# Denominators of a lookup-table convolution by tensor tiles of 128 rows and 32 columns, with the two accumulator banks told apart by the set of logits

## The chip, the cores and the metric

The kernel runs on one core of one Trainium2 chip. The metric is the device time of one execution in microseconds, the median of three runs. A profiled execution on the same chip gives the trace from which all durations here are read.

## The reference

The input is 16 images of 256 channels with 28 x 28 pixels. After a group normalization (32 groups) it passes twice through a "lookup" convolution, each with a batch normalization behind it; then a gate per channel (squeeze and excitation), a residual sum, a rectifier and the outer residual sum follow. The convolution is what matters here:

```python
def amm_conv3x3(x, centroids, w_sub):              # centroids: C x k x s = 256 x 16 x 9
    p = patches(x, 3, 3)                           # B, n, C, s: nine taps of each channel
    d = sum(p * p) - 2 * einsum('bncs,cks->bnck', p, centroids) + sum(centroids * centroids)
    attn = softmax(-d, axis=-1)                    # over the k = 16 centroids of a channel
    lut = einsum('cks,cso->cko', centroids, w_sub)
    return einsum('bnck,cko->bno', attn, lut)
```

For each channel and pixel a softmax over 16 centroids is taken. Its weighted sum of the centroids has nine taps, and these go through an ordinary matrix product with `w_sub`. The kernel computes it in that order: logits, exponentials, numerators for nine taps and a denominator, the quotient, and the product over channels and taps. All of it is fp32.

## The kernel before, in words

**Blocks.** The work is cut into 128 blocks: two layers, 16 images, and for each image two halves of the channels (128 each) by two halves of the rows (14 rows, N = 392 pixels). A block holds four sets of logits, `mm` = 0 to 3, and each set has four groups `i` with 128 partitions: 8 channels with 16 centroids each. So one block has 4 x 4 x 8 = 128 channels.

**Steps of a block.** `logits` (line 613) makes a set of logits with 16 matmuls on tiles of 32 rows and 32 columns. `exps` (line 624, ScalarE) writes the exponentials `e`. `num_b` (line 678) makes, from all four sets, the denominators and the ninth tap's numerators in the accumulator pair `nb`. `num_a` (line 664) makes the other eight taps in the pairs `na`, one pair for each set. `product` (line 748) multiplies the scaled numerators `qp` (eight taps) and `qo` (ninth tap) with the weights into `acc`, with full 128x128 tiles.

**The denominators.** `nb` has two banks. In both, 32 rows belong to each group `i`: 16 of them are ninth-tap numerators and 16 are denominators. Which bank has its numerators in the lower 16 and which in the upper 16 rows differs, so that each bank gives one half of each. `split_r` (line 688, ScalarE) takes the upper rows of bank 0 with a mask. `join_r` (line 692, VectorE) adds the lower rows of bank 1: together these are the denominators `r`. `recip_dve` (line 706) inverts them. `split_q` and `join_q` (lines 698 and 703) collect the ninth tap's numerators from the other halves in the same way. `spread` (lines 717 and 721) copies the reciprocals to the rows of the numerators with a shuffle in 32 partitions whose pattern `mask_of` gives. `scale_a`, `copy_a` and `scale_q` then multiply.

Before the change the two banks are told apart by the half of the 128 rows, that is, by the channels of a group: rows 0 to 63 of the exponentials go to bank 0, rows 64 to 127 to bank 1, and each bank accumulates over all four sets. `rows_of` gives the place of each channel in these rows. The constants, the mask tables and the table that places the second layer's weights are laid out by it.

**Order.** Each engine works through its own list, which the program writes by hand: `at(step, sub, ...)` puts a call at a place, and the calls are issued in order of these places. For most blocks TensorE's order in a double step is logits, denominators, logits, products, logits, numerators, logits, products. The denominators thus lie between two logits stages. Accumulator pairs come from a ring of four pairs. In the blocks of the second layer with the first channel half the first set takes a longer way with a subtracted maximum.

Of the kernel before, what the change touches and what calls it, by code (L numbers as in the profile page):

```python
# [23 lines left out]
N = RT * W  # L24
# [57 lines left out]

def rows_of(m, c, a):
    r, c4, mm = c >> 1, 2 * (c & 1) + a, m & 3
    return r, c4, mm, 16 * r + 4 * mm + c4, 16 * (1 - r) + 4 * mm + c4


@with_exitstack
def kernel(
# [22 lines left out]
    nc = tc.nc  # L112
# [19 lines left out]
    def fixed(u, kind):  # L132
        return None if u["step"] is None else EARLY.get((kind, u["step"] // 2))

    def banks(name, step=None, role=None, tag=None):
        if tag is not None:
            pass
        elif step is None:
            spin[0] = (spin[0] + 1) % 4
            tag = spin[0]  # L140
        else:
            tag = (role - step // 2) % 4
        return p_ring.tile([P, 2, 512], F32, tag=f"ps{tag}", name=name)
# [4 lines left out]
    def after(u, n):  # L148
        return None if u["step"] is None else u["step"] + n
# [49 lines left out]
    wts = {}  # L199
# [472 lines left out]
    def num_b(u):  # L672
        bs = banks("nb", after(u, 2), ROLES["nb"], fixed(u, "nb"))
        for mm in range(4):
            es = u["e", mm]
            for i in range(4):
                for r in range(2):
                    nc.tensor.matmul(  # L678
                        bs[32 * i : 32 * i + 32, r, :N],
                        lhsT=wts["cwb", u["hh"]][64 * r : 64 * r + 64, mm, i, :],  # L680
                        rhs=es[64 * r : 64 * r + 64, i, :],
                        start=(mm == 0), stop=(mm == 3),
                    )
        u["nb"] = bs

    def split_r(u):
# [21 lines left out]
    def mask_of(k):  # L708
        if k == 8:
            return [(xx + 16) % 32 for xx in range(32)]  # L710
        mm, r = divmod(k, 2)
        return [16 * (1 - r) + 4 * mm + (xx >> 3) for xx in range(32)]

    def spread(u, mm):
        if mm == 4:
            rb = rpool.tile([P, N], F32, tag="rb1", name="rb1", bufs=1)
            nc.vector.stream_shuffle(rb, u["r"], mask_of(8))  # L717
        else:
            rb = rpool.tile([P, 2, N], F32, tag="rb", name="rb", bufs=4)
            for r in range(2):  # L720
                nc.vector.stream_shuffle(rb[:, r, :], u["r"], mask_of(2 * mm + r))  # L721
        u["rb", mm] = rb
# [527 lines left out]
    for j, u in enumerate(blocks):  # L1250
# [3 lines left out]
        for p in range(2):  # L1254
# [6 lines left out]
            for q in range(2):  # L1261
                mm = 2 * p + q
# [11 lines left out]
        kept = () if j == 1 else SLOT_MM[1 : 4 if wide_next(j) or j == 0 else 2 : 2]  # L1274
        g = 2 * j + 1 + (j > 2)
        at(g, 1.0, num_b, u)
        at(g, 1.05, split_r, u)
        at(g, 1.2 if j > 1 else 1.055, join_r, u)
# [158 lines left out]
    for o in range(2):  # L1437
# [7 lines left out]
        for part in range(2):  # L1445
            c = 40 + 8 * o + 2 * part
# [5 lines left out]
    for part in range(3):  # L1452
        c = (68, 70, 76)[part]
# [96 lines left out]
    with tc.If(rv > 0):  # L1550
        with tc.For_i(0, B, 1) as it:
# [14 lines left out]
            for l in range(2):  # L1566
# [6 lines left out]
                for t2 in range(2):  # L1573
                    us = []
                    for hh in range(2):
                        u = {"l": l, "b": B, "t": t2, "hh": hh, "w": 0, "step": None}
                        for k in range(5):
                            u["qi", k] = hh if k == 4 else 4 * hh + k
                        us.append(u)
                        for mm in range(4):  # L1580
                            if mm % 2 == 0:
                                u["pt", mm // 2] = pts[mm // 2]
                                patches(u, mm // 2)
                            logits(u, mm)
                            wide_copy(u, mm)
                            wide_turn(u, mm)
                            wide_max(u, mm)
                            wide_sub(u, mm)
                            wide_back(u, mm)
                            wide_exp(u, mm)  # L1590
                        num_b(u)
                        split_r(u)
                        join_r(u)
                        split_q(u)
                        join_q(u)
                        recip_dve(u)
                        spread(u, 4)
                        scale_q(u, 4)
                        for mm in range(4):
                            spread(u, mm)  # L1600
                            num_a(u, mm)
                            scale_a(u, mm)
# [23 lines left out]
def _lay_out(inputs):  # L1626
# [15 lines left out]
    for c0 in range(ch):  # L1642
        i, a, m, c = digits(c0)
        r, c4, mm, rn, rs = rows_of(m, c, a)
        hh = m >> 2
        ka = slice(32 * c + 16 * a, 32 * c + 16 * a + 16)
        for s in range(S):
            wd[32 * i + 16 * a + tap_row(s), m, c, 16 * a : 16 * a + 16] = cent[c0][:, s]
        cwa[ka, m, i, 8 * c4 : 8 * c4 + 8] = cent[c0][:, :8]
        cwb[ka, m, i, rn] = cent[c0][:, 8]  # L1650
        cwb[ka, m, i, rs] = 1.0
        ws[32 * i + 8 * c4 : 32 * i + 8 * c4 + 8, NS * hh + 2 * mm + r] = wsub[c0, :8]
        ws[32 * i + rn, NS * hh + 8] = wsub[c0, 8]
        konst[ka, 3 + c4] = 1.0
        konst[ka, 48 + 32 * mm + rn] = 1.0
        konst[ka, 176 + 32 * mm + rs] = 1.0
        wa = (2 * m + r) * 16 + 4 * i + c4
        ids[c0] = (c0, (2 * c + a) * 32 + 4 * m + i, 2 * wa, 2 * wa + 1, hh * P + 32 * i + rn, 2 * c0, 2 * c0 + 1)
# [66 lines left out]
```

## Time and profile before

| what | value |
|---|---|
| time, median of 3 runs | 2607.75 us (2605.92 to 2608.51) |
| the profiled execution: span | 2606.2 us |
| granted TensorE clock | 0.999 |
| TensorE matmuls busy | 2591.2 us (99%) |
| VectorE, ScalarE, GpSimd busy | 1776.6, 1371.7, 1905.6 us |
| DMA | 372.07 MB, mean 143 GB/s |
| line 748 `product`, records of matmuls with qp and `wall` | 3088 records, 1097.5 us |
| line 613 `logits` | 15872 records, 469.0 us |
| line 664 `num_a` | 8192 records, 376.5 us |
| line 678 `num_b` | 8192 records, 375.2 us |

The profiled execution's span of 2606.2 us, from its first to its last instruction, is the only time known of it; it lies 1.5 us below the median of the runs. An fp32 matmul appears as two records in the trace, one for each of its two passes. Records of several tiles overlap in time, and "busy" is the length of their union. In a row of the timeline stand the start, the length of the union, the engine, the line, the operands, the tile (64*32 is 64 rows by 32 columns of the array) and the number of records. A row of the groups ends with busy time, the mean duration of one record in ns, and the engine's idle time before the group's records with what ended it.

### The profile page before, as it was taken

How to read it: one execution, taken by the hardware profiler on the slowest of the kernel's cores; microseconds unless marked ns; L12 is line 12 of the kernel's file. 1: busy time of each engine (PE TensorE's matmuls, PEld its weight loads, DVE VectorE, ACT ScalarE, POOL GpSimd, SP SyncE). 2: the span in 40 equal slices, each digit the busy share in tenths (PEclk: the TensorE clock that was granted, in tenths of full speed). 3: DMA queues.
4: the chain of work that ended last, by engine and by line, in shares of the span. 5: the costliest groups of instructions: out<-in, count | busy, mean ns of one | idle time of the engine just before them, and what ended most of it. 6: DMA issues, size and time to landing. Idle time of an engine off the chain costs nothing.

```text
span 2606.2 us, 85832 instructions
## 1 busy us (share of the span) xinstructions
PE 2591.2 (99%) x37026; PEld 1273.2 (49%) x37026; DVE 1776.6 (68%) x3797; ACT 1371.7 (53%) x1913; POOL 1905.6 (73%) x1341
## 2 busy tenths in 40 slices
PE   8999999999999999999999999999999999999999
PEld 4444455444454444544444444444444444444445
DVE  8766656666657666566676767766776667767676
ACT  6444444444444445444445555555555655555565
POOL 6687666776567776667666887878878787787786
PEclk9999999999999999999999999999999999999999
DMA  7556656565545575564664444444344444444442
GB/s 228 166 131 184 195 166 187 160 168 170 163 141 147 157 194 173 165 172 134 176 169 103 109 112 127 119 119 120 101 126 128 118 116 112 115 124 128 117 104 66
DMA packets 213288, 372.07 MB, mean 143 GB/s; under 512 B 29496, under 2 KB 183528, under 8 KB 212328
## 3 DMA queue, kind: packets, MB, share of 16 engines
q1 hardware_dynamic: 206584, 333.75, 47.6%
q0 software_dynamic: 6176, 32.66, 3.5%
q8 instruction: 295, 4.83, 0.8%
q14 instruction: 89, 0.73, 0.1%
q10 hardware_dynamic: 144, 0.10, 0.0%
HBM read 288.46 MB, written 77.95 MB: 141 GB/s over the span
## 4 chain that ended last, share of the span: by engine, by line
PE 99%; ACT 0%; POOL 0%; DVE 0%; issue 0%; DMA 0%; POOLq 0%; ACTq 0%
PE acc L748 52%; PE lg L613 17%; PE na L664 14%; PE nb L678 14%; ACT e L624 0%; PE sep L1049 0%; POOL qp L757 0%; PE sep L1041 0%; DMA xt<-in_x 0%; PE tap L392 0%; PE sqp L374 0%; PE sqp L343 0%; POOL qp L729 0%; PE gnp L534 0%; PE gnp L551 0%
## 5 line engine op out<-in xcount | busy, mean ns | idle before, releaser
L748 PE MATMUL acc<-qp,wall 128*128 128x392 f32 (+1 forms) x3088 | 1097.5, 498 | 0.3 <-POOL qp L757 0.2
L624 ACT ACTIVATE e<-lg 128x784 f32<-128x784 f32 x960 | 737.8, 820 | 635.2 <-PE lg L613 632.0
L757 POOL TENSOR_TENSOR qp<-qp,qp 128x784 f32<-128x784 f32 x512 | 943.7, 1867 | 152.0 <-DVE qp L740 151.6
L748 PEld LDWEIGHTS acc<-qp,wall 128*128 128x128 f32 x3088 | 567.4, 190 | 504.8 <-issue 53.6
L721 DVE STREAM_SHUFFLE rb<-r 128x392 f32<-128x392 f32 x1024 | 551.5, 606 | 0.0
L613 PE MATMUL lg<-pt,wd 32*32 32x392 f32 x15872 | 469.0, 499 | 0.2
L692 DVE SCALAR_TENSOR_TENSOR r<-nb,kst,r 128x392 f32<-128x392 f32 x128 | 80.1, 626 | 447.6 <-ACT r L688 447.6
L664 PE MATMUL na<-e,cwa 64*32 64x392 f32 x8192 | 376.5, 493 | 0.0
L740 DVE TENSOR_TENSOR qp<-na,rb 128x784 f32<-128x784 f32 x352 | 334.0, 972 | 62.2 <-PE na L664 50.3
L678 PE MATMUL nb<-e,cwb 64*32 64x392 f32 x8192 | 375.2, 492 | 0.1
L729 POOL TENSOR_TENSOR qo<-qo,rb 128x392 f32<-128x392 f32 x128 | 132.5, 1035 | 297.0 <-DVE rb L717 296.2
L706 DVE RECIPROCAL r<-r 128x392 f32<-128x392 f32 x128 | 333.2, 2603 | 4.4
L729 POOL TENSOR_TENSOR qp<-qp,rb 128x784 f32<-128x784 f32 x160 | 295.7, 1858 | 2.9
L678 PEld LDWEIGHTS nb<-e,cwb 64*32 64x32 f32 x8192 | 191.5, 106 | 174.7 <-issue 24.5
L664 PEld LDWEIGHTS na<-e,cwa 64*32 64x32 f32 x8192 | 183.8, 106 | 184.0 <-issue 74.8
L613 PEld LDWEIGHTS lg<-pt,wd 32*32 32x32 f32 x15872 | 116.4, 103 | 266.6 <-issue 238.3
L748 PE MATMUL acc<-qp,w_A 128*128 128x392 f32 x512 | 182.4, 499 | 0.0
L688 ACT ACTIVATE r<-nb,kst 128x392 f32<-128x392 f32 x128 | 86.7, 678 | 165.5 <-PE nb L678 162.3
L648 POOL TENSOR_TENSOR z<-z,mx 128x1568 f32<-128x1568 f32 x32 | 91.8, 2869 | 94.8 <-DVE mx L642 94.8
L748 PE MATMUL acc<-qo,wall 128*128 128x392 f32 (+1 forms) x386 | 157.9, 491 | 0.0
L734 ACT COPY qp<-na 128x784 f32<-128x784 f32 x160 | 130.0, 813 | 23.6 <-PE na L664 22.1
L748 PEld LDWEIGHTS acc<-qp,w_A 128*128 128x128 f32 x512 | 94.6, 190 | 82.5 <-DVE qp L740 19.8
(241 smaller groups left out, 1706.4 us busy)
## 6 DMA issues: line engine op xcount, KB each, us to landing
pt<-home SPq DMA_DIRECT2D x744, 209.0 KB
pt<-home SPq DMA_DIRECT2D x744, 104.5 KB
home<-xpad SPq DMA_DIRECT2D x30, 899.0 KB
xt<-in_x SPq DMA_DIRECT2D x30, 784.0 KB
out_dram<-y SPq DMA_DIRECT2D x31, 392.0 KB
pt<-in_p SPq DMA_DIRECT2D x6, 784.0 KB
d_wS<-st SPq DMA_DIRECT2D x12, 192.0 KB
wall<-d_wS SPq DMA_DIRECT2D x4, 576.0 KB
```

Source lines behind the costliest of these rows:

```text
L613: nc.tensor.matmul(bk[32 * c : 32 * c + 32, :N].rearrange("p (r w) -> p r w", w=W), lhsT=(wx[u["hh"]] if early(u) else wts["wd", u["hh"]]) ...
L624: nc.scalar.activation(eg[:, 2 * i : 2 * i + 2, :], bk[:, :, :N], AF.Exp, scale=2.0)
L648: nc.gpsimd.tensor_tensor(zk, zk, mx.unsqueeze(2).to_broadcast([P, N // 4, K]), ALU.subtract)
L664: nc.tensor.matmul(bs[32 * i : 32 * i + 32, r, :N], lhsT=wts["cwa", u["hh"]][64 * r : 64 * r + 64, mm, i, :], rhs=es[64 * r : 64 * r + 64, ...
L678: nc.tensor.matmul(bs[32 * i : 32 * i + 32, r, :N], lhsT=wts["cwb", u["hh"]][64 * r : 64 * r + 64, mm, i, :], rhs=es[64 * r : 64 * r + 64, ...
L706: nc.vector.reciprocal(u["r"], u["r"])
L721: nc.vector.stream_shuffle(rb[:, r, :], u["r"], mask_of(2 * mm + r))
L729: nc.gpsimd.tensor_tensor(q, q, u.pop(("rb", mm)), ALU.mult)
L734: nc.scalar.copy(pair(u, mm), u.pop(("na", mm))[:, :, :N])
L740: nc.vector.tensor_mul(pair(u, mm), u.pop(("na", mm))[:, :, :N], rb)
L748: nc.tensor.matmul(accs[key][:, : cols[1] - cols[0]], lhsT=wl[w][:, k, :], rhs=us["q", k][:, cols[0] : cols[1]], start=first and n == 0, s ...
L757: nc.gpsimd.tensor_tensor(pair(out_u, mm), pair(in0, mm), pair(in1, mm), ALU.subtract)
```

## The change

`num_b` issues one matmul with all 128 rows for each set and group, where it issued two with 64 rows each. Sets 0 and 1 go to bank 0, sets 2 and 3 to bank 1, and each bank accumulates over its two sets. `rows_of` and `mask_of` lay out rows and shuffle patterns for this. The masks of `split_r`, `join_r`, `split_q` and `join_q`, the number of shuffles and the order of the calls stay.

```diff
 def rows_of(m, c, a):
     r, c4, mm = c >> 1, 2 * (c & 1) + a, m & 3
-    return r, c4, mm, 16 * r + 4 * mm + c4, 16 * (1 - r) + 4 * mm + c4
+    rn = 8 * mm + 2 * c + a
+    return r, c4, mm, rn, (rn + 16) % 32
...
         for mm in range(4):
             es = u["e", mm]
             for i in range(4):
-                for r in range(2):
-                    nc.tensor.matmul(
-                        bs[32 * i : 32 * i + 32, r, :N],
-                        lhsT=wts["cwb", u["hh"]][64 * r : 64 * r + 64, mm, i, :],
-                        rhs=es[64 * r : 64 * r + 64, i, :],
-                        start=(mm == 0), stop=(mm == 3),
-                    )
+                nc.tensor.matmul(
+                    bs[32 * i : 32 * i + 32, mm >> 1, :N],
+                    lhsT=wts["cwb", u["hh"]][:, mm, i, :], rhs=es[:, i, :],
+                    start=mm % 2 == 0, stop=mm % 2 == 1,
+                )
         u["nb"] = bs
...
         mm, r = divmod(k, 2)
-        return [16 * (1 - r) + 4 * mm + (xx >> 3) for xx in range(32)]
+        return [(8 * mm + 4 * r + (xx >> 3) + 16) % 32 for xx in range(32)]
```

## The prediction

> **What bounds the kernel now.** I read the page's busy shares and chain first, then the waits of TensorE, then the groups by line for the denominators (line 678), then the timeline around one of their stages.
>
> ```profile
> PE 2591.2 (99%) x37026; PEld 1273.2 (49%) x37026; DVE 1776.6 (68%) x3797; ACT 1371.7 (53%) x1913; POOL 1905.6 (73%) x1341
> PE acc L748 52%; PE lg L613 17%; PE na L664 14%; PE nb L678 14%; ACT e L624 0%; PE sep L1049 0%; POOL qp L757 0%; PE sep L1041 0%; DMA xt<-in_x 0%; PE tap L392 0%; PE sqp L374 0%; PE sqp L343 0%; POOL qp L729 0%; PE gnp L534 0%; PE gnp L551 0%
> ...
> PE gnp L436 <- DVE gn_mv L425: 5.6, 1, 5.6
> ...
> PE acc L748 <- POOL qp L757: 0.2, 1, 0.2
> ```
>
> TensorE is busy 2591.2 of 2606.2 us, and the chain that ends last lies on it almost throughout; 14% of it are the denominators. The last two rows are the first and the last of eight in TensorE's own waits. The largest, 5.6 us, falls before the first denominators; the other seven are 0.7 us or less. So a change pays only through the time that TensorE itself takes for the edited stage, and whatever another engine gains or loses up to several us per block stays under that cover.
>
> ```profile
> L678 PE MATMUL nb<-e,cwb x8192: 486/489/515, 21.0 to 2563.7; 64*32 64x392 f32 x200
> 1020.37 0.94 PE L613 MATMUL lg<-pt,wd 32*32 32x392 f32 x32
> 1021.24 2.92 PE L678 MATMUL nb<-e,cwb 64*32 64x392 f32 x64
> 1024.09 0.94 PE L613 MATMUL lg<-pt,wd 32*32 32x392 f32 x32
> ```
>
> The first row gives 8192 records: 128 blocks with 64 each, two passes of each of 32 fp32 matmuls, 0.49 us long in the median and up to 0.51 in a first pass. One stage goes from 1021.24 to the next stage's start at 1024.09: 2.85 us, with logits on both sides. Windows that end inside this stage show how it is built:
>
> ```profile
> 1021.24 0.55 PE L678 MATMUL nb<-e,cwb 64*32 64x392 f32 x4
> 1021.24 0.62 PE L678 MATMUL nb<-e,cwb 64*32 64x392 f32 x8
> 1021.24 0.94 PE L678 MATMUL nb<-e,cwb 64*32 64x392 f32 x16
> 1021.24 1.27 PE L678 MATMUL nb<-e,cwb 64*32 64x392 f32 x24
> ...
> 1023.57 0.59 PE L678 MATMUL nb<-e,cwb 64*32 64x392 f32 x8
> 1037.63 0.53 PE L678 MATMUL nb<-e,cwb 64*32 64x392 f32 x4
> 1037.63 0.56 PE L678 MATMUL nb<-e,cwb 64*32 64x392 f32 x8
> ```
>
> Eight records, one on each tile, take 0.62 us together, sixteen 0.94, twenty-four 1.27. So eight 64x32 tiles run side by side, and each further pass on all of them costs 0.33 us. A stage is eight such passes. Besides them it holds two fixed pieces: the ladder, by which the eighth tile starts after the first (0.62 less one record of 0.51: 0.11 us), and the emptying of the array before the next shape (the last eight start at 1023.57 and the logits at 1024.09: 0.52, less the ladder's 0.11, so 0.41). At 1037.63 the ladder is shorter, 0.56 less 0.51: 0.05.
>
> **The change, part by part.** *The matmuls.* Per block 32 matmuls of 64 rows become 16 of 128 rows: 32 records in place of 64. But four tiles of 128x32 fill the array where eight of 64x32 did, so the passes stay at eight: 16 x 2 records over 4 tiles, 8 x 0.33. Halving the instructions therefore does not halve the stage. What shrinks is the ladder, from eight tiles to four. If the steps stay as they are, four tiles end where the first four do today: 0.62 - 0.55 = 0.07 us less per stage. With even steps of 0.11/7 = 0.015 it is four steps less, 0.06. I take 0.065. In the short form it is 0.56 - 0.53 = 0.03.
>
> How many stages have which form?
>
> ```profile
> 1000.00:2000.00 1000.00, 146.25 (x3208) 74.92 (x3204) 1.00 0.50 135
> ```
>
> In this row (line 678 alone; the stretch, its length, then the busy time of TensorE with its records) 3208 records are 50.1 stages, and 146.25 / 50.1 = 2.92 us each, the long form's busy time. Short ones are rare; I take 8 of 128, an estimate. The sum: 120 x 0.065 + 8 x 0.03 = 8.0 us. From the profiled 2606.2 us that leaves 2598.2. The three runs have a median of 2607.75, 1.5 us above that span, so the forecast is 2599.8.
>
> The trace has no neighbouring 128x32 tiles, so the step between them is unknown. Low end: the short form's step, 0.05/7 = 0.007, three of them 0.02, a gain of 0.09 per long stage and 0.03 per short one, 11.0 us in all, 2596.7. High end: twice the long step, as the rows double, 3 x 0.03 = 0.09, a gain of 0.02, 2.6 us, 2605.2. I take the middle one because the step already differs between two stages of the same shape: the shape does not set it, the arrival of instructions does, and that should not slow down with half as many.
>
> *Weight loads.* They fall from 64 to 32 per block. Per load:
>
> ```profile
> L678 PEld LDWEIGHTS nb<-e,cwb 64*32 64x32 f32 x8192 | 191.5, 106 | 174.7 <-issue 24.5 <-ACT y L779 10.2 <-ACT se_gt L1055 8.9
> L1041 PEld LDWEIGHTS sep<-ysum,w_sb 128*32 128x32 f32 x68 | 3.3, 110 | 8.9 <-issue 8.4 <-DVE ok L1208 0.6
> L748 PEld LDWEIGHTS acc<-qp,wall 128*128 128x128 f32 x3088 | 567.4, 190 | 504.8 <-issue 53.6 <-POOL qp L757 21.3 <-DVE qp L740 20.4
> 1021.24 0.24 PEld L678 LDWEIGHTS nb<-e,cwb 64*32 64x32 f32 x16 [0.64 <-ACT hpad L779]
> 1008.24 1.48 PE L748 MATMUL acc<-qp,wall 128*128 128x392 f32 x4
> ```
>
> A 128x32 load is already in the program, in the gate's small matmuls: 110 ns against 106. Loads lie under matmuls: sixteen of a denominator stage are through after 0.24 us, while the second passes that need half of them start only at 0.94 - 0.62 = 0.32 us or later. I cost them at nothing; the cover is the 0.33 us of the pass before.
>
> The Trainium skill speaks against this cover ("TensorE: Matmul & The Clock Gate", Part 3, The mechanism): a weight load overlaps matmuls in flight "only when row_grp differs", and four tiles of 128 rows share all row groups. By that rule the sum would not be a gain of 8.0 us but the loss of the second rival below. The trace does not bear it out: the products use all rows, each load takes 190 ns, and yet four records fit in 1.48 us, (1.48 - 0.49) / 3 = 0.33 us apart.
>
> *The denominators' earlier half.* Bank 0 now closes after sets 0 and 1, and its copy on ScalarE (line 688) needs nothing more.
>
> ```profile
> 1021.36 1.54 ACT L624 ACTIVATE e<-lg 128x784 f32<-128x784 f32 x2 [0.35 <-PE lg L613]
> 1024.21 0.68 ACT L688 ACTIVATE r<-nb,kst 128x392 f32<-128x392 f32 x1 [1.31 <-PE nb L678]
> 1024.92 0.62 DVE L692 SCALAR_TENSOR_TENSOR r<-nb,kst,r 128x392 f32<-128x392 f32 x1 [8.65 <-ACT r L688]
> ```
>
> Bank 0 is whole after four passes, about 1021.24 + 0.35 + 2 x 0.33 + 0.04 + 0.49 = 1022.8. ScalarE is in the exponentials until 1022.9, so the copy can move from 1024.21 to 1022.9; the join on VectorE then waits for bank 1, ready at about 1024.1, not for 1024.92. The reciprocal chain comes up to 0.8 us earlier per block. If the wait still covers both banks, nothing moves. Both are worth nothing at TensorE, which waits for no reciprocal in the list of its waits; the seven short waits together would be under 5 us and none names this chain. No wait is added, and the first write into bank 1 moves from the first matmuls to the ninth, which only loosens its wait.
>
> *The rest* has one answer, nothing: the spreading keeps its 1024 shuffles with other masks, the constants change their contents and not their sizes, and the scattered rows of the ninth tap's weights go to other places in transfers of the same count. The numerators keep their 64x32 tiles.
>
> **Rivals.** *The ladder's step doubles with the rows.* For: the profile has no 128x32 neighbours. Against: steps of 0.007 and 0.015 in one shape. Time 2605.2, 0.1% less, which is inside what a measurement of this kernel can tell from no change (0.2%, 5.2 us).
>
> *Loads are exposed.* If a load has to stand ahead of its matmul on every pass, a stage pays 8 x 0.11 = 0.88 us, 128 stages 112.6, less 8.0: 2712.4, slower. It decides from 0.065 / 8 = 0.008 us per pass on. For it: four loads of one row group have never stood beside each other here at full height. Against: the 16 loads in 0.24 us and the products above.
>
> *The column tiles take turns.* If only one 128x32 tile streams at a time, a stage has 32 passes instead of 8: 24 x 0.33 = 7.9 us more, 1014 in all, less 8.0: 3614. Two at a time give 8 more passes, 2.64 us, 338 in all: 2938. A fifth of one extra pass per stage is enough to turn the sign. For it: the only 128x32 tile in the trace stands alone. Against: the logits, where all four columns of a row group stream different data at once.
>
> ```profile
> 1024.09 0.61 PE L613 MATMUL lg<-pt,wd 32*32 32x392 f32 x16
> ```
>
> Sixteen tiles, four columns by four rows, take 0.61 us together, so four column streams over all 128 rows are sustained. The Trainium skill lists 128x32 as a shape with four tiles ("TensorEngine Tiling (Array Packing)", Available Configurations); no run here shows it.
>
> **How the numbers follow.** The shorter ladder 0.74; the doubled step 0.13; exposed loads 0.07; turns 0.06. The first lies over 0.2% faster with its ends of 0.06 to 0.09 per stage, the second is the same, the last two are slower: 0.74, 0.13, 0.13. The predicted time is the first's, 2599.8. The range takes both ends of the step, 2596.7 and 2605.2, and 1.5 us at either end, which is how far the runs lie from the span: 2595.2 to 2606.7. It leaves out the two slower rivals, 0.13.
>
> **What would show it.** Right: 4096 records of 128x32 at line 678, still about 0.49 us each, four of them in 0.55 us and eight in 0.88; a stage of 2.78 to 2.79 us from its first start to the next stage; the numerators still 2.85 and the products unchanged; the copy at line 688 over 1 us ahead of where it stood, with no gain from that. Wrong: passes more than 0.33 us apart (loads or turns), a first group of four that takes 0.60 us (the step), or a wait of TensorE that today's list does not have.

## The result, and the profile after

| | before | after |
|---|---|---|
| median time | 2607.52 us (2603.88 to 2608.51, 5 runs) | 2596.91 us (2596.11 to 2598.35, 5 runs) |
| ratio | | 0.9965 (95%: 0.9954 to 0.9976) |
| span of the profiled execution | 2606.2 us | 2595.0 us |

The change makes the kernel 0.35% faster, 9.1 us of 2607.5, where 8.0 us were forecast. By the medians it is 10.6, by the two profiled spans 11.2 us.

First the page of the changed kernel: busy times and the groups of denominators (line 678) and numerators (line 665 there). Each group's row ends with the number of records, their joint busy time and the mean of one in ns.

```profile
PE 2579.0 (99%) x32930; PEld 1215.7 (47%) x32930; DVE 1775.9 (68%) x3797; ACT 1371.8 (53%) x1913; POOL 1906.5 (73%) x1341
...
L665 PE MATMUL na<-e,cwa 64*32 64x392 f32 x8192 | 373.9, 492 | 0.0
L678 PE MATMUL nb<-e,cwb 128*32 128x392 f32 x4096 | 366.3, 495 | 0.1
...
L678 PEld LDWEIGHTS nb<-e,cwb 128*32 128x32 f32 x4096 | 135.1, 109 | 222.2 <-issue 154.4
```

TensorE lost 12.2 us of busy time; the other engines changed by less than 1 us each. The denominators have 4096 records for 8192, each about as long as before (495 against 492 ns on average), and yet their busy time fell only from 375.2 to 366.3 us: half the instructions, the same eight passes. That is 8.9 of the 12.2 us. Another 2.6 us are the numerators', from 376.5 to 373.9, which the change leaves alone; the part on the prediction's total comes back to them. A weight load took 109 ns, close to the 110 of the gate's load.

Next the timeline of TensorE around one such stage of the changed kernel, whole and through windows that end inside it.

```profile
1014.96 0.94 PE L614 MATMUL lg<-pt,wd 32*32 32x392 f32 x32
1015.83 2.86 PE L678 MATMUL nb<-e,cwb 128*32 128x392 f32 x32
1018.62 0.94 PE L614 MATMUL lg<-pt,wd 32*32 32x392 f32 x32
...
1015.83 0.55 PE L678 MATMUL nb<-e,cwb 128*32 128x392 f32 x4
1015.83 0.88 PE L678 MATMUL nb<-e,cwb 128*32 128x392 f32 x8
```

And the stretch from 1000 to 2000 us for line 678 alone: the stretch, its length, the busy time of TensorE and of its weight loads, each with the number of records, then the clock and the DMA.

```profile
1000.00:2000.00 1000.00, 142.87 (x1600) 52.75 (x1600) 1.00 0.51 136
```

The stage goes from 1015.83 to 1018.62, 2.79 us for 2.85. Its first four records take 0.55 us together: four 128x32 tiles run side by side, and the fourth starts 0.04 us after the first, as did the fourth of eight before. The next four add 0.33 us, one pass. In the stretch a stage is busy 142.87 / 50 = 2.86 us, against 2.92: 0.06 us less, and 128 x 0.06 = 7.7 us. Read to the nanosecond, the median stage falls from 2851 to 2788 ns and its ladder from 106 to 39.

Now the timeline of ScalarE and VectorE around the same stage of the changed kernel:

```profile
1015.96 1.54 ACT L625 ACTIVATE e<-lg 128x784 f32<-128x784 f32 x2 [0.36 <-PE lg L614]
1018.74 0.68 ACT L687 ACTIVATE r<-nb,kst 128x392 f32<-128x392 f32 x1 [1.25 <-PE nb L678]
1019.45 0.62 DVE L691 SCALAR_TENSOR_TENSOR r<-nb,kst,r 128x392 f32<-128x392 f32 x1 [8.59 <-ACT r L687]
```

ScalarE is through with the exponentials at 1017.5, and bank 0 is whole at about 1017.4. Still the copy waits 1.25 us, to 0.12 us behind the stage's end. It did not move.

### The profile page after: what moved, and what is told of

It is laid out like the page before. It is cut to its first block, busy times and chain, and to the rows that moved or that the text cites. A ratio compares the mean times of both kernels' runs of the same rounds, so it can differ in the third digit from the quotient of the medians.

```text
span 2595.0 us, 77640 instructions
## 1 busy us (share of the span) xinstructions
PE 2579.0 (99%) x32930; PEld 1215.7 (47%) x32930; DVE 1775.9 (68%) x3797; ACT 1371.8 (53%) x1913; POOL 1906.5 (73%) x1341
## 4 chain that ended last, share of the span: by engine, by line
PE 98%; DVE 1%; ACT 0%; POOL 0%; issue 0%; DMA 0%; POOLq 0%; ACTq 0%
PE acc L747 53%; PE lg L614 17%; PE na L665 14%; PE nb L678 14%; ACT e L625 0%; PE sep L1048 0%; POOL qp L756 0%; PE sep L1040 0%; DMA xt<-in_x 0%; DVE rb L720 0%; DVE r L705 0%; PE tap L393 0%; PE sqp L375 0%; PE sqp L344 0%; POOL qp L728 0%
## 5 line engine op out<-in xcount | busy, mean ns | idle before, releaser
L665 PE MATMUL na<-e,cwa 64*32 64x392 f32 x8192 | 373.9, 492 | 0.0
L678 PE MATMUL nb<-e,cwb 128*32 128x392 f32 x4096 | 366.3, 495 | 0.1
L678 PEld LDWEIGHTS nb<-e,cwb 128*32 128x32 f32 x4096 | 135.1, 109 | 222.2 <-issue 154.4
```

The lines of the kernel that those rows point to most:

```text
L665: nc.tensor.matmul(bs[32 * i : 32 * i + 32, r, :N], lhsT=wts["cwa", u["hh"]][64 * r : 64 * r + 64, mm, i, :], rhs=es[64 * r : 64 * r + 64, ...
L678: nc.tensor.matmul(bs[32 * i : 32 * i + 32, mm >> 1, :N], lhsT=wts["cwb", u["hh"]][:, mm, i, :], rhs=es[:, i, :], start=mm % 2 == 0, stop= ...
```

## Experiments

The kernel before ran beside each of these on the same chip; ratios are to it. Where no ratio is given, the kernel was executed once. For comparison, the changed kernel has 0.9965.

**A second trace of the kernel before.** No edit.

> The kernel before once more, for a second trace. If the stalls in mid-stage (TensorE without an instruction, 0.2 to 0.9 us each, some dozen in the first trace, about 5 us in all) are fixed by the program, they stand at the same blocks; if they are a matter of the execution, at others, with a similar sum. The regular stages stay at 2.85 us for denominators and numerators.

Measured: 2604.58 us, span 2603.1, 3.1 us less than the first trace. The groups of its page:

```profile
L664 PE MATMUL na<-e,cwa 64*32 64x392 f32 x8192 | 374.5, 492 | 0.2 <-issue 0.2
L678 PE MATMUL nb<-e,cwb 64*32 64x392 f32 x8192 | 374.0, 492 | 0.1
```

A logits stage takes 0.94 us in the timeline where nothing stops it. One that does stall, in the first trace:

```profile
1035.87 1.83 PE L613 MATMUL lg<-pt,wd 32*32 32x392 f32 x32
```

And two in the timeline of the second trace:

```profile
548.77 1.74 PE L613 MATMUL lg<-pt,wd 32*32 32x392 f32 x32
1032.49 1.81 PE L613 MATMUL lg<-pt,wd 32*32 32x392 f32 x32
```

Neither outcome that was expected: some stalls come back at the same stage (1.83 and 1.81 us, the block near 1035), some do not, and their sum changes. Summed over all stages between 80 and 2500 us, as what each is longer than the median of its kind with the same neighbours, they are 5.1 us in the first trace and 3.1 in the second; 2.7, 2.9 and 4.1 in the traces of the changed kernel and of the next two experiments. Single spans therefore differ by 2 or 3 us without any edit, and 11.2 us from one pair of them overstates the gain.

**Bank 0 closes last.** From the changed kernel:

```diff
-        for mm in range(4):
+        for mm in (2, 0, 3, 1):
             es = u["e", mm]
```

> The changed kernel, with the four sets of the denominators issued in the order 2, 0, 3, 1, so that bank 0 is whole only with the stage's last matmuls and its copy on ScalarE can start no earlier than in the kernel before. Theory A (the whole gain is TensorE's: a ladder of four tiles in place of eight, and less besides that does not hang on the copy): stage 2.79 us, time as the changed kernel's, 2597 within 2 us, and the 1 us that the numerators of the first block gained at the start stays. Theory B (the earlier copy of bank 0 helps): the copy falls back to over 1 us after ScalarE's exponentials, the early blocks lose what they gained and the time goes up by 1 to 3 us, to 2598 to 2600.

Measured: 2595.64 us against 2604.30, ratio 0.9965 (0.9952 to 0.9979). The timeline of TensorE and of ScalarE in this kernel, a stage and what follows it:

```profile
1015.38 2.86 PE L678 MATMUL nb<-e,cwb 128*32 128x392 f32 x32
1018.16 0.94 PE L614 MATMUL lg<-pt,wd 32*32 32x392 f32 x32
...
1018.28 0.68 ACT L687 ACTIVATE r<-nb,kst 128x392 f32<-128x392 f32 x1 [1.25 <-PE nb L678]
```

The time is the changed kernel's, as theory A has it. But the copy stands 0.12 us behind the stage here as there, so this run took nothing away: it shows that the order of the sets is free, and not what an earlier copy is worth. The 1 us at the start stayed as well: the first stage of numerators goes from 28.64 to 31.43, 2.79 us, against 4.11 in the first trace of before.

**The numerators with their row halves outside.** From the changed kernel:

```diff
-        for i in range(4):
-            for r in range(2):
+        for r in range(2):
+            for i in range(4):
                 nc.tensor.matmul(
                     bs[32 * i : 32 * i + 32, r, :N],
                     lhsT=wts["cwa", u["hh"]][64 * r : 64 * r + 64, mm, i, :],
```

> The changed kernel with the numerators' 64x32 matmuls issued with the row halves outside and the four groups inside; same tiles, same passes. Theory A (the ladder's step is the arrival of instructions at the array, 0.0166 us for each fp32 matmul): the ladder stays at 0.11 us, the stage at 2.85, the time at 2597 within 2. Rival (the step is set by which tile follows which, 7 ns within a group of columns and more from one group to the next, or the reverse): the ladder of the numerators changes to 0.05 or to 0.15 and the time by 7 us either way.

Measured: 2595.83 us against 2604.30, ratio 0.9966 (0.9952 to 0.9980). The first eight numerator records of a stage in this kernel's timeline:

```profile
1026.11 0.62 PE L665 MATMUL na<-e,cwa 64*32 64x392 f32 x8
```

0.62 us, a ladder of 0.11, as before. For these tiles, which one follows which does not set the step; the rival falls.

**Half of the logits moved behind the denominators**, in the kernel before and in the changed one. Of set 0, groups 2 and 3 are made behind the denominators:

```diff
-    def logits(u, mm):
-        bs = []
+    def logits(u, mm, half=None):
+        bs = u.pop(("lg", mm)) if half == 1 else []
...
-        for i in range(4):
+        for i in range(4) if half is None else range(2 * half, 2 * half + 2):
...
+                if mm == 0 and j >= 4 and not wide:
+                    for h in range(2):
+                        at(cl, 1.09 if h else sub, logits, u, mm, h)
+                        at(cl, 1.095 if h else sub + 0.01, exps_half, u, mm, h)
+                    continue
```

> The kernel before, with half of the logits of set 0 (groups 2 and 3, 8 of the 16 matmuls ahead of the denominators) moved behind the denominators, in all blocks but the first four and those that subtract the maximum. It costs passes of its own (about 0.6 us in each such block), so its time is not the question. Theory A (the array's queue holds the logits until they are done, and what comes behind them arrives at 0.0166 us for each matmul): with half as many ahead the first eight denominator matmuls are in the queue, ladder 0.05 us and stage 2.79 in these blocks; 0.11 and 2.85 in the others; the numerators keep 0.11. Rival (the change of shape after logits, or the shape itself, makes the step): 0.11 and 2.85 in all of them.

> The same move of half the logits in the changed kernel. Theory A: the ladder of four tiles falls from 0.04 to 0.02 us and the stage from 2.79 to 2.77 us in these blocks. Rival: 0.04 and 2.79 everywhere.

Measured: 2690.56 and 2685.17 us, 86 us or more over the kernels without the move: some 0.95 us for each of the 91 halved blocks, more than the 0.6 that was expected. What counts are the ladders. The timeline of the edited kernel before: the halved logits, the first eight denominators behind them, and the first eight numerators of another stage with all sixteen logits ahead.

```profile
1016.71 0.89 PE L613 MATMUL lg<-pt,wd 32*32 32x392 f32 x16
1017.52 0.56 PE L684 MATMUL nb<-e,cwb 64*32 64x392 f32 x8
1029.18 0.62 PE L670 MATMUL na<-e,cwa 64*32 64x392 f32 x8
```

And the first four denominators behind halved logits in the timeline of the edited changed kernel:

```profile
1014.84 0.54 PE L684 MATMUL nb<-e,cwb 128*32 128x392 f32 x4
```

Same shape, same neighbour, same kernel: with eight logits matmuls ahead, eight tiles are under way in 0.56 us, with sixteen in 0.62. Read to the nanosecond from the trace, all 91 halved stages have a median ladder of 47 ns and a length of 2794 ns, the 34 with sixteen logits ahead 106 and 2851. In the changed kernel the halved stages have 20 ns and 2776, the others 39 and 2787.

The halved logits differ from the whole ones in one thing more: they leave half of the array's rows without work. That is not the reason, as one stage of numerators in the timeline of the changed kernel shows. It stands straight behind products, which use all 128 rows, and its first eight records take 0.56 us too:

```profile
56.92 4.22 PE L747 MATMUL acc<-qp,wall 128*128 128x392 f32 x12
60.97 0.82 PE L747 MATMUL acc<-qo,wall 128*128 128x392 f32 x2
61.72 0.56 PE L665 MATMUL na<-e,cwa 64*32 64x392 f32 x8
```

So the ladder is set by what stands ahead, not by the shape or its change. That the queue keeps the logits until they are done is the explanation that fits; the trace does not show the queue.

**The matmuls cut in two halves of 196 pixels**, from the changed kernel, first with the two halves of a tile one after the other, then with the four tiles inside. Both have 64 records per block again.

```diff
             for i in range(4):
+                for c0 in (0, N // 2):       # second kernel: this loop outside, i inside
                     nc.tensor.matmul(
-                    bs[32 * i : 32 * i + 32, mm >> 1, :N],
-                    lhsT=wts["cwb", u["hh"]][:, mm, i, :], rhs=es[:, i, :],
-                    start=mm % 2 == 0, stop=mm % 2 == 1,
+                        bs[32 * i : 32 * i + 32, mm >> 1, c0 : c0 + N // 2],
+                        lhsT=wts["cwb", u["hh"]][:, mm, i, :], rhs=es[:, i, c0 : c0 + N // 2],
+                        start=mm % 2 == 0 and c0 == 0, stop=mm % 2 == 1 and c0 > 0,
```

> The changed kernel with every 128x32 denominator matmul cut into two of 196 pixels: again 32 matmuls and 64 records per block, as before the change, but on four tiles. Theory A (the ladder is what the change shortened): a record costs some 2 to 3 ns beside its pixels, 8 x 0.003 us per stage, 3 us in all; stage 2.81 us, ladder still 0.04 us or less, ratio to the kernel before 0.9975 to 0.998. Theory B (half as many instructions is what pays): ratio 1.000, as before the change. Theory C (stalls in mid-stage come with the fetching of instructions): besides A's 3 us, instruction packets back from 263 to about 295 and some 2 us more stalls.

> The halved matmuls of 196 pixels once more, with the pixel halves outside and the four tiles inside: the same 64 records per block on the same four tiles, but the second tile's first matmul arrives second and not third. Theory A (ladder: arrival of one matmul for each tile before all tiles run): ladder back from 0.09 to 0.04 us, stage 2861 - 50 = 2.81 us, 6.4 us less than with the halves inside, ratio to the kernel before 0.9975 to 0.9985; what is left over the changed kernel's stage, 0.02 us, is 8 more records on each tile. Theory B (the number of instructions): stage and time as with the halves inside, ratio 1.000.

Measured with the halves inside: 2605.72 us against 2604.50, ratio 1.0004 (0.9995 to 1.0013). Measured with them outside: 2599.32 against 2604.30, ratio 0.9979 (0.9970 to 0.9988). The row of the instruction queue on the page (packets, MB, share) is the same in both:

```profile
q8 instruction: 295, 4.83, 0.8%
```

A stage's first four records, the stage and the next stage's start in the timeline, with the halves inside:

```profile
1019.56 0.44 PE L679 MATMUL nb<-e,cwb 128*32 128x196 f32 x4
1019.56 2.93 PE L679 MATMUL nb<-e,cwb 128*32 128x196 f32 x64
1022.42 0.94 PE L614 MATMUL lg<-pt,wd 32*32 32x392 f32 x32
```

And with the halves outside:

```profile
1018.52 0.39 PE L679 MATMUL nb<-e,cwb 128*32 128x196 f32 x4
1018.52 2.88 PE L679 MATMUL nb<-e,cwb 128*32 128x196 f32 x64
1021.32 0.94 PE L614 MATMUL lg<-pt,wd 32*32 32x392 f32 x32
```

The first of these runs fell on theory B's number, and theory A's expectation was wrong by 6 us. Its trace says why. With the halves inside, each tile's first matmul is every second one, and the first four records take 0.44 us instead of 0.39: the ladder is 0.05 us longer. I had overlooked that the order changes what stands ahead of a tile. The second run tells the theories apart: same instructions, same tiles, same traffic of the instruction queue, and with the order alone the stage falls from 2.86 to 2.80 us and the time by 0.25%. Theory B, that the number of instructions is what pays, falls for these stages. What remains over the changed kernel, 0.02 us per stage in the medians (2807 against 2788 ns), is the price of eight more records on each tile, 2.4 ns each. Theory C is not borne out between 80 and 2500 us: with 295 packets the stalls, summed as above, were 2.0 and 3.9 us here and 5.1 and 3.1 in the kernel before, with 263 they were 2.7 to 4.1. The first 80 us are not in these sums; there the two kinds of kernels do differ, as told at the end of the next section.

**The copy between the sets**, from the changed kernel; `num_b` takes the sets as an argument there and makes the pair of banks with the first two:

```diff
...
-        at(g, 1.0, num_b, u)
-        at(g, 1.05, split_r, u)
+        at(g, 1.0, num_b, u, (0, 1))
+        at(g, 1.002, split_r, u)
+        at(g, 1.004, num_b, u, (2, 3))
```

> The changed kernel with the copy of bank 0 on ScalarE (split_r) issued between the denominators of sets 0 and 1 and those of sets 2 and 3, so that its wait can end with bank 0. In the changed kernel it waits for the whole pair, to 0.12 us behind the stage. Theory A (the copy's place is worth nothing, since TensorE waits for no reciprocal): if the wait covers bank 0 alone, the copy starts with the end of ScalarE's exponentials, some 1.2 us earlier, the join on VectorE 0.7 us earlier, TensorE's stage stays at 2.79 us and the ratio to the kernel before at 0.9965 within 0.001. Theory B (the earlier reciprocal is worth time): 1 us or more below the changed kernel. Rival to both (the pair is guarded as a whole): sets 2 and 3 wait on TensorE for the copy, some 1 us per block, 128 us in all, ratio 1.04 to 1.05.

Measured: 2730.79 us against 2605.34, ratio 1.0483 (1.0468 to 1.0497). The row of TensorE's waits (total, times, longest):

```profile
PE nb L678 <- ACT r L687: 108.0, 128, 2.1
```

One stage in this kernel's timeline, on TensorE and on ScalarE:

```profile
1002.01 1.54 PE L678 MATMUL nb<-e,cwb 128*32 128x392 f32 x16
1004.33 1.53 PE L678 MATMUL nb<-e,cwb 128*32 128x392 f32 x16 [0.78 <-ACT r L687]
...
1003.60 0.68 ACT L687 ACTIVATE r<-nb,kst 128x392 f32<-128x392 f32 x1
```

The rival of both theories held. The pair of banks is guarded as one tile: whoever reads bank 0 waits for every write issued before, whichever bank it went to, and the next write to bank 1 waits for that read, 128 times, 108 us idle in all, in a time 125 us over that of the kernel before (what else it lost was not followed up). So the copy's place behind the stage in the changed kernel is the guard's. Whether an earlier copy would pay stays untried, and so does a tile for each bank, which might allow it.

## Why the prediction was right, point by point

*The bound.* Right. TensorE is 99% busy in both; its stage became 0.06 us shorter and the time followed. That several us per block on another engine would stay covered was not tested.

*Eight passes in place of eight, no halving.* Right: 0.33 us from four to eight records, and records about as long as before. The four column tiles do not take turns: their first records take 0.55 us together.

*The ladder.* Right in place and size: 0.55 us for the first four tiles, 2.79 us for the stage, 7.7 us in all against the 8.0 of the sum. The reason given, that arrival sets the step and not the shape, is borne out by the halved logits and by the order of the halved matmuls; the doubled step did not occur. The steps are not even, though: in both kernels the second tile starts 7 ns after the first and each later one 15 to 17 ns after the one before, so the ladder lost 67 ns (106 less 39), as the first of the two estimates has it, and the stage 63. Five of the 128 stages before had the short form, where 8 were taken. The numerators, untouched, kept 2.85 us.

*Weight loads at nothing.* Right: 109 ns each, and passes 0.33 us apart. The rule of the Trainium skill ("TensorE: Matmul & The Clock Gate", Part 3, The mechanism), that a load overlaps matmuls in flight only when their row groups differ, is not what these stages show: their four tiles share all row groups, and no pass grew. The prediction set that sentence against the cover and left out another of the same section, by which a load into the background weight buffer is pulled ahead as well; whether that is the case here, no trace shows.

*The copy of bank 0.* The mark named for it, over 1 us earlier, failed. Of the two cases in the text, "if the wait still covers both banks, nothing moves" is the one that holds. It was priced at nothing either way, so the sum did not suffer. That nothing would follow from an earlier copy stays argued.

*No wait is added.* Not to the letter. The list of TensorE's waits in the changed kernel has two rows that the list before lacks, which the prediction had named as a sign of being wrong:

```profile
PE lg L614 <- PE nb L678: 0.6, 1, 0.6
PE tap L393 <- DVE qp L739: 0.2, 1, 0.2
```

Each occurs once, at 37.30 and 31.91 us of the span, in stages that come earlier than before. The kernel in which bank 0 closes last has neither. They are 0.8 us at the start, and the regular stages have no new wait.

*The total.* 9.1 us measured by ratio against 8.0, and the interval of 6.3 to 12.0 us holds both. The two variants above that keep the changed denominators whole, with bank 0 last and with the numerators' halves outside, gain 8.7 and 8.5 us by their medians, so the missing 1 us is no more than such comparisons differ by. Part of it may lie at the start, which the sum did not look at. Read from the traces, the same stage of numerators on TensorE begins at 81.0 and 80.2 us in the two traces of before, at 79.8, 79.1 and 79.4 in three kernels with 32 records per block, and at 81.5 in both kernels with cut matmuls and 64 records again. The ladder explains at most some 0.2 us of that. Much of it is one stage, the first of the numerators, with what follows it on TensorE. In the timeline of before:

```profile
29.38 4.18 PE L664 MATMUL na<-e,cwa 64*32 64x392 f32 x64
33.49 1.13 PE L392 MATMUL tap<-wd,nhalf_sb 128*128 128x256 f32 x4
```

And of the changed kernel:

```profile
28.89 2.86 PE L665 MATMUL na<-e,cwa 64*32 64x392 f32 x64
31.91 1.13 PE L393 MATMUL tap<-wd,nhalf_sb 128*128 128x256 f32 x4 [0.16 <-DVE qp L739]
```

Neither its instructions nor its tiles were changed, and yet it takes 4.1 us in the one and 3.0 in the other. From its start to the next stage it is 3.7 to 4.9 us in all five traces of kernels with 64 records of denominators per block, the two cut ones among them, and 2.8 to 3.0 in all five with 32. So here the number of instructions goes with some 1 to 2 us, once, where a regular stage paid 19 ns for twice as many. Why is not shown. The mid-stage stalls vary too much from trace to trace to be put down to the change.

## What to carry to other kernels

Halving the instructions of a tiled matmul stage buys little by itself if the number of passes over the array stays (19 ns of 2807 per stage here): look at how many records one pass holds and how far apart passes start. What a stage of many small tiles pays beside its passes is the ladder to its last tile (106 ns for eight tiles here, 39 for four), and that is set by how many matmuls must arrive before every tile has one: use fewer, taller tiles where the layout allows, and issue the first matmul of each tile before the second of any. A result in one bank of a pair was not free early here, because the pair is guarded as one tile; a tile for each bank was not tried.

## What the runs showed that I had not expected

- The step of the ladder depends on what stands ahead: 47 ns for eight tiles behind 8 logits matmuls, 106 behind 16, same shape.
- TensorE stalls in mid-stage with no wait on record, up to 1.6 us, several per execution, some at the same stage of the program in repeated traces (near 1035 us in both of before). Their sum of 2 to 5 us is a fifth to over half of the 9.1 us measured here. Their cause was not shown.
- The first stage of the numerators, which the change does not touch, became 1 us shorter (4.1 and 3.8 us in the two traces of before, 2.8 to 3.0 with half as many records of denominators).
- Cutting a 128x32 matmul of 392 pixels in two cost only 2.4 ns per record, as long as the order of the tiles was kept.
